# A selective-scan kernel whose per-output adding transfers are issued at other steps and in another order of chunks

## The chip, the cores and the metric

The kernel runs on one core of one Trainium2 chip, as one launch. The metric is the device time of that core in microseconds (us). The kernel before took 9282.05 us, the median of three runs that lay between 9277.97 and 9287.36.

## The reference, cut to what matters

Two layers run one after the other. The first is a linear attention with a layer norm and a residual. The second is a four-direction selective scan with one state per channel, and the change lies in its last part. With 8 images, 256 inner channels (two chunks of 128 partitions) and L = 128 x 128 places, it computes in essence:

```python
xs = jnp.stack([xf, xf[..., ::-1], xt, xt[..., ::-1]], axis=1)       # four directions
dA = jnp.exp(delta * A); xc = dA * xc + delta * u * B; y = xc * C     # scan over L
return y + u * Dv                                                     # the D term
y = y0 + y1 + y2 + y3                    # the directions, turned back to one order
yz = y * silu(z)                         # gate
yn = gamma * (yz - mu) / jnp.sqrt(var + 1e-05) + beta
out = yn @ Wout
```

`u * Dv` is the D term. Because images and directions are mixed by a reshape, the four scans that sum to one output belong to two to four different images, and the D terms of an output depend only on `o // 4`: there are two D sums, each shared by four outputs.

## The kernel before, in words

There are three parts: `layer0`, `layer1_front` and `layer1_scan`. The front computes u, the rows that the scans need, and the two D sums, and leaves them in HBM: u in `ubs`, the rows in `xps`, the gate z in `zs`, the D sums in `gs`. The change touches only `layer1_scan`, which starts at about 4520 us of the profile.

**Units, places and steps.** The scans are cut into 512 units of 1024 positions: for each of 8 outputs o, four scans (four *places*) of 16 units each (`NCH = 16`). A Python function `step(n)` writes out by hand the order in which every engine works, and an order of this kind is kept on every engine (`in_order`). In step n the unit n is weighed and scanned, unit n-1 is multiplied by its C and added to the sum `y`, and the loads of unit n+2 are issued. `y` is a tile of 128 x 2 x 16384 floats that stays in SBUF; the four scans of an output are summed in it. The first place of an output writes `y` (L979), the other three add to it, one half on DVE (L993 or L989, then L1001), the other on GpSimd (L982 on DVE, then L1009).

**Counting steps.** In this text the steps of the last place of an output are numbered 0 to 15, and those of the next output's first place 16 to 31. Step k begins on DVE with the product of the unit before.

**What a step holds.** In the last three places of an output:
- DVE: L993/L989, L1001, L982 and two scans (L959 or L961).
- GpSimd (POOL): two products of u and the softened delta (`weigh`, L951), two additions into `y` (L1009).
- ACT: two softplus (L938) and two exponentials (L942).
- SP issues the loads: rows (L916, L917) and u (`ubt`, L923), both for the unit two steps later.

**Leaving.** While the first place of the next output runs (steps 16 to 31, the `leaving` table), the finished sum leaves in chunks of 1024 positions, one a step: it is multiplied by z (`gate`, L1029, one half on GpSimd in the step before, the other on DVE), squared (L1032), its moments are taken on PE (L1042, L1054), the deviation is made on GpSimd (L1066, L1067), it is projected on PE (L1074), scaled on DVE into a tile `r` (L1080), and stored by SP (`out<-r`, L1084). `r` has two buffers, one for each half of a chunk. So L1080 of one step must wait until the two stores of the step before have landed. SP also issues the loads of z (L1025) in these steps, from step 17 to step 29 for chunks 3 to 15. In the last output there is no next scan, and steps 16 to 32 are a tail with the leaving alone.

**The adding transfers.** The D sum of an output comes from HBM by 16 transfers of 1 MB, each of which adds its data to one chunk of `y`:

```python
def add_d(o, m):
    v = y[:, :, m * CH : m * CH + CH]
    nc.gpsimd.dma_start(v, gs[o // 4].rearrange("c p l -> p c l")[:, :, m * CH : m * CH + CH], accum_op=ALU.add)
```

They are issued by GpSimd (L907) as the last thing of a step, where the table `summed` has an entry. A chunk may be added at any time between the first write of `y` (place 0) and its gate, apart from the units that work on it at that moment; the table decides. Before, the chunk that is the j-th to leave was added in step 3 + (3j + 1) // 2, that is, in steps 3, 5, 6, 8, 9, 11, 12, 14, 15 of the last place and in steps 17, 18, 20, 21, 23, 24, 26 of the next: two in three steps, in the order in which the chunks leave.

Of the kernel before, what the change touches and what calls it, by code (L numbers as in the profile page):

```python
# [32 lines left out]
NCH = L // CH  # L33
# [714 lines left out]
def layer1_scan(ctx: ExitStack, tc, ubs, xps, zs, gs, dtw, dtb, a_log, gamma, beta, w_out, out):  # L748
# [36 lines left out]
    for dst, src, rows in ((wparts, dtw.rearrange("k r d -> r k d"), R), (bparts, dtb.rearrange("o (k d) -> o k d", d=D2), 1)):  # L785
        x = wp.tile([rows, K, D2], F32, name="w32", tag="sp", bufs=2)
        nc.sync.dma_start(x, src)
        q = wp.tile([rows, 3, K, D2], BF16, name="w16", tag="h", bufs=2)
# [298 lines left out]


    leaving, summed, fetched, weighed = {}, {}, {}, {}
    for o in range(B):  # L1090
        n = (o + 1) * K * NCH
        for j in range(NCH):
            e = o, NCH - 1 - j if o % 2 == 1 else j
            leaving[n + j] = e
            fetched[n + j - (2 if j > 2 else NCH + 4)] = e
            summed[n - NCH + 3 + (3 * j + 1) // 2] = e
        n -= K * NCH
        weighed[n + NCH + 1] = n + 2 * NCH
        weighed[n + NCH + 8] = n + 3 * NCH
        if o + 1 < B:  # L1100
            weighed[n + 2 * NCH + 1] = n + 4 * NCH
            weighed[n + 3 * NCH + 1] = n + 5 * NCH
# [104 lines left out]
@with_exitstack  # L1207
def tile_kernel(ctx: ExitStack, tc, a, out):
    dram = ctx.enter_context(tc.tile_pool(name="dram", bufs=1, space=DRAM))
    x1 = dram.tile([B, P, L], F32, name="x1")  # L1210
    ubs = dram.tile([B, 2, NC2, P, L], F32, name="ubs")
    xds = dram.tile([B, R + 2, L], F32, name="xds")
    xps = dram.tile([B, 2, 3, R + 2, L], BF16, name="xps")
    zs = dram.tile([B, NC2, P, L], F32, name="zs")
    gs = dram.tile([2, NC2, P, L], F32, name="gs")
    layer0(
        tc, a["x"], a["L0_conv_w_qkv"], a["L0_conv_w_out"], a["L0_conv_b_out"],
        a["L0_conv_gamma"], a["L0_conv_beta"], a["L1_conv_Win"], x1, zs,
    )
    layer1_front(  # L1220
        tc, x1, a["L1_conv_Win"], a["L1_conv_conv_w"], a["L1_conv_conv_b"], a["L1_conv_Wxproj"],
        a["L1_conv_D_param"], ubs, xds, xps, gs,
    )
    layer1_scan(
        tc, ubs, xps, zs, gs, a["L1_conv_dt_weight"], a["L1_conv_dt_bias"], a["L1_conv_A_log"],
        a["L1_conv_gamma"], a["L1_conv_beta"], a["L1_conv_Wout"], out,
    )
# [40 lines left out]
```

## Time and profile before

| what | value |
|---|---|
| median of three runs | 9282.05 us |
| the profiled execution's own time | 9288.8 us |
| its span, first to last instruction | 9287.0 us |
| DVE busy | 7986.4 us (86%) |
| POOL busy | 7316.7 us (79%) |
| ACT busy | 7097.3 us (76%) |
| adding transfers into `y` (L907) | 128 of 1024 KB, median 10.3 us from issue to landing |
| waits of L1080 for `out<-r` | 80.7 us, 32 times |
| L951 (POOL) | 1024 of 2389 ns |
| L959 and L961 (DVE scans) | 1024 of 2331 and 2330 ns |

The profiled execution took 9288.8 us, of which 1.8 us lie around the span; it is 6.75 us above the median. A line of the profile's list of groups names source line, engine, operation, tiles (written<-read), shapes and count, then busy time and the mean duration, then the idle time before, with what ended it. A line of the timeline gives start and duration in us, engine, line, operation, tiles, count, and in brackets the idle time before it with its releaser. In a table of windows each engine has its busy us and count; the last three columns are the granted TensorE clock, the mean busy share of the 16 DMA engines and GB/s.

### The profile page before, as it was taken

The numbers are of one execution on the slowest core, as the hardware profiler recorded it, in microseconds if no ns is written. First come the engines' busy times: TensorE is split into PE (matmuls) and PEld (weight loads), VectorE is DVE, ScalarE is ACT, GpSimd is POOL, SyncE is SP. The second block draws the span as 40 slices with busy tenths as digits, with TensorE's granted clock in tenths as the row PEclk, the third lists the DMA queues.
The fourth block names the chain that finished last, engine by engine and source line by source line (L and its number), as shares of the span: only waits on it lengthen the run. The fifth ranks groups of instructions, "written<-read, shape, count | busy, mean of one in ns | idle before, by whom it ended". The sixth has DMA issues, their size and how long they took to land.

```text
span 9287.0 us, 91371 instructions
## 1 busy us (share of the span) xinstructions
PE 6364.4 (69%) x24512; PEld 3119.9 (34%) x24512; DVE 7986.4 (86%) x7953; ACT 7097.3 (76%) x8066; POOL 7316.7 (79%) x4684
## 2 busy tenths in 40 slices
PE   8899998988899999999334636346363463643636
PEld 5555555554333333333102304113041140311403
DVE  6667666774799999999799999999999999999996
ACT  5555555658789999999687787888888878888784
POOL 3446444564689988888599899999999989999897
PEclk9999999999999999999555657557575575755757
DMA  1322333223478788888658659577594775957757
GB/s 76 145 84 97 135 120 145 80 100 136 153 247 249 253 244 244 245 245 243 200 156 226 209 180 261 155 222 227 175 269 154 220 221 169 269 161 208 234 167 214
DMA packets 934770, 1750.67 MB, mean 189 GB/s; under 512 B 150228, under 2 KB 376148, under 8 KB 926064
## 3 DMA queue, kind: packets, MB, share of 16 engines
q1 hardware_dynamic: 873328, 1509.92, 48.0%
q0 software_dynamic: 60928, 234.90, 13.6%
q8 instruction: 200, 3.28, 0.1%
q14 instruction: 314, 2.57, 0.1%
HBM read 1052.36 MB, written 692.12 MB: 188 GB/s over the span
## 4 chain that ended last, share of the span: by engine, by line
DVE 36%; PE 5%; DMA 3%; issue 3%; POOL 2%; ACT 1%; DVEq 0%; SPq 0%; POOLq 0%; ACTq 0%
DVE h L961 10%; DVE h L959 10%; DVE y L1001 4%; DVE h L982 4%; DVE px L989 3%; PE px L1074 3%; DMA out<-r 3%; DVE r L1080 2%; DVE px L993 1%; POOL h L951 1%; PE pm L1042 1%; PE pq L1054 0%; PE pc L967 0%; POOL y L1009 0%; POOL z L1029 0%
## 5 line engine op out<-in xcount | busy, mean ns | idle before, releaser
L951 POOL TENSOR_TENSOR h<-ubt,sp 128x1024 f32<-128x1024 f32 x1024 | 2416.6, 2389 | 374.9 <-DMA rows<-xps 92.6
L934 PE MATMUL px<-rows,dtw 128*128 128x512 bf16 x2048 | 956.3, 566 | 2277.8 <-DVE y L1001 1073.2
L534 DVE SCALAR_TENSOR_TENSOR acc<-xb,cw,acc 128x1024 f32<-128x1024 f32 x1024 | 1320.3, 1289 | 133.6 <-ACT xb L502 89.8
L526 POOL TENSOR_TENSOR tap<-tap 128x1024 f32<-128x1024 f32 x512 | 1223.6, 2393 | 243.7 <-ACT tap L524 220.4
L938 ACT ACTIVATE sp<-px 128x1024 f32<-128x1024 f32 x1024 | 1046.7, 1024 | 436.4 <-PE px L934 413.8
L934 PEld LDWEIGHTS <-dtw 128*128 128x128 bf16 x2048 | 168.8, 110 | 3100.8 <-issue 1031.3
L961 DVE TENSOR_TENSOR_SCAN h<-px,h 128x1024 f32<-128x1024 f32 x512 | 1177.4, 2331 | 31.6 <-ACT px L942 15.4
L959 DVE TENSOR_TENSOR_SCAN h<-px,h 128x1024 f32<-128x1024 f32 x512 | 1178.1, 2330 | 22.4 <-POOL h L951 18.5
L1009 POOL TENSOR_TENSOR y<-y,h 128x512 f32<-128x512 f32 x768 | 1159.4, 1553 | 4.3 <-DVE h L982 4.3
L942 ACT ACTIVATE px<-sp,sa 128x1024 f32<-128x1024 f32 x1024 | 1110.4, 1109 | 6.1
L515 PE MATMUL acc<-xi,wt 128*128 128x512 f32 x2048 | 937.6, 600 | 53.6 <-ACT ures L539 53.6
L524 ACT ACTIVATE tap<-xb,cw 128x1024 f32<-128x1024 f32 x768 | 837.3, 1139 | 15.2 <-POOL xb L499 15.1
L282 POOL TENSOR_TENSOR q<-q,qs 128x512 f32<-128x512 f32 x256 | 271.6, 1061 | 697.0 <-DVE qs L281 697.0
L938 ACT ACT_TABLE_LOAD x512 | 656.9, 1283 | 164.6 <-PE px L934 162.7
L942 ACT ACT_TABLE_LOAD x512 | 656.9, 1283 | 9.2
L1074 PEld LDWEIGHTS px<-wg,z 128*128 128x128 f32 x4096 | 588.5, 229 | 113.3 <-issue 107.1
L1074 PE MATMUL px<-wg,z 128*128 128x128 f32 x4096 | 586.9, 312 | 0.0
L967 PE MATMUL pc<-rows,csel 128*128 128x512 bf16 x1024 | 520.0, 588 | 74.8 <-DVE rstd L1062 70.9
L515 PEld LDWEIGHTS acc<-xi,wt 128*128 128x128 f32 x2048 | 374.7, 189 | 573.9 <-issue 411.5
L488 PE MATMUL pxb<-xi,wi 128*128 128x512 f32 x1024 | 495.6, 606 | 2.1 <-ACT xb L497 2.1
L298 ACT ACTIVATE sq<-o 128x512 f32<-128x512 f32 x256 | 161.2, 630 | 420.3 <-DVE o L296 419.1
L1001 DVE TENSOR_TENSOR y<-y,px 128x1024 f32<-128x1024 f32 x384 | 468.5, 1220 | 14.4
(153 smaller groups left out, 15037.9 us busy)
## 6 DMA issues: line engine op xcount, KB each, us to landing
ubt<-ubs SPq DMA_DIRECT2D x1024, 512.0 KB
zs<-z SPq DMA_DIRECT2D x512, 256.0 KB
ubs<-ures SPq DMA_DIRECT2D x256, 512.0 KB
ubs<-turned SPq DMA_DIRECT2D x256, 512.0 KB
z<-zs SPq DMA_DIRECT2D x256, 512.0 KB
y<-gs POOLq DMA_DIRECT2D x128, 1024.0 KB, 10.3
gs<-du POOLq DMA_DIRECT2D x96, 1024.0 KB, 8.6
rows<-xps SPq DMA_DIRECT2D x1536, 60.0 KB
```

The source lines that it names most:

```text
L515: nc.tensor.matmul(acc[:, s, :], wt[:, j, c, :], x, start=(j == 0), stop=(j == len(ON_PE) - 1))
L526: nc.gpsimd.tensor_tensor(sums[n, c], sums[n, c], t, ALU.add)
L534: nc.vector.scalar_tensor_tensor(acc, at(n, c, *d), weight(n, c, *d), acc, ALU.mult, ALU.add)
L934: nc.tensor.matmul(p[:, hf * 512 : hf * 512 + 512], sl.dw[:, c * P : c * P + P], src, start=True, stop=True)
L938: nc.scalar.activation(t, da[n, c], AF.Softplus)
L942: nc.scalar.activation(da[n, c], sp[n, c], AF.Exp, scale=sa[:, sl.s, c : c + 1])
L951: nc.gpsimd.tensor_tensor(h, u, t, ALU.mult)
L959: nc.vector.tensor_tensor_scan(e[:, ::-1], x[:, ::-1], e[:, ::-1], start, ALU.mult, ALU.add)
L961: nc.vector.tensor_tensor_scan(e, x, e, start, ALU.mult, ALU.add)
L1001: nc.vector.tensor_tensor(v, v, ts.pop(n), ALU.add)
L1009: nc.gpsimd.tensor_tensor(v[:, c], v[:, c], h[:, c], ALU.add)
L1074: nc.tensor.matmul(po[:, w, :], z[:, c, w * H : w * H + H], wg[:, c, :], start=(c == 0), stop=(c == NC2 - 1))
```

## The change

Only the table `summed` changes. The chunks that leave 11th to 16th (j = 10 to 15) are added first, then those with j = 0 to 9. With q as the rank in this new order, the step is 1 + 4q // 3. So the adds go out in steps 1, 2, 3, 5, 6, 7 (j = 10 to 15), 9, 10, 11, 13, 14, 15, and 17, 18, 19, 21 (j = 0 to 9): three in four steps. Twelve lie in the last place and four in the next output's first place, where it was nine and seven. The transfers themselves, their number and their size stay, and so does the order on every engine but GpSimd.

```diff
     leaving, summed, fetched, weighed = {}, {}, {}, {}
+    LATE = 10
     for o in range(B):
         n = (o + 1) * K * NCH
         for j in range(NCH):
             e = o, NCH - 1 - j if o % 2 == 1 else j
             leaving[n + j] = e
             fetched[n + j - (2 if j > 2 else NCH + 4)] = e
-            summed[n - NCH + 3 + (3 * j + 1) // 2] = e
+            q = j - LATE if j >= LATE else NCH - LATE + j
+            summed[n - NCH + 1 + 4 * q // 3] = e
```

## The prediction, as it went on record

> **What bounds the kernel now.** I read the page first: busy shares, the chain that ended last, the DMA queues. The change touches only the scan part (from about 4520 us on).
>
> ```profile
> span 9287.0 us, 91371 instructions
> ...
> q1 hardware_dynamic: 873328, 1509.92, 48.0%
> q0 software_dynamic: 60928, 234.90, 13.6%
> ...
> DVE 36%; PE 5%; DMA 3%; issue 3%; POOL 2%; ACT 1%; DVEq 0%; SPq 0%; POOLq 0%; ACTq 0%
> ...
> y<-gs POOLq DMA_DIRECT2D x128, 1024.0 KB, 10.3
> ```
>
> DVE leads the chain, with 3% of DMA behind it. The queue rows give a price. q0 carries 128 + 96 adding transfers of 1 MB: 13.6% of 9287 us is 1263 us of all 16 DMA engines, so one add holds them for 5.64 us. q1 moves 1510 MB in 48.0%, 2.95 us a MB. An added MB costs about twice a plain one.
>
> Next the timeline of POOL and DVE in one last place, to see if an add costs time there.
>
> ```profile
> 4943.66 4.66 POOL L951 TENSOR_TENSOR h<-ubt,sp 128x1024 f32<-128x1024 f32 x2 [1.08 <-DMA rows<-xps]
> 4948.28 2.48 POOL L1009 TENSOR_TENSOR y<-y,h 128x512 f32<-128x512 f32 x2
> 4950.72 1.18 POOL L907 DMA_DIRECT2D y<-gs  x1
> 4951.90 4.69 POOL L951 TENSOR_TENSOR h<-ubt,sp 128x1024 f32<-128x1024 f32 x2
> 4956.53 2.50 POOL L1009 TENSOR_TENSOR y<-y,h 128x512 f32<-128x512 f32 x2
> 4958.96 1.23 POOL L907 DMA_DIRECT2D y<-gs  x1
> 4960.12 4.76 POOL L951 TENSOR_TENSOR h<-ubt,sp 128x1024 f32<-128x1024 f32 x2
> ```
>
> A step there is 8.22 us (start to start), set by DVE: its products follow each other without idle time. POOL needs 4.66 + 2.48 = 7.14 us and idles 1.08. With an add (1.2 us) it fills the step exactly: 8.24 and 8.22 us from L951 to L951. Adds are free for DVE here, but POOL has nothing left.
>
> Then windows: places without adds, a last place with adds, a first place with adds, its end without.
>
> ```profile
> 5245.00:5375.00 130.00, 46.75 (x96) 9.04 (x96) 127.89 (x80) 106.46 (x95) 122.85 (x63) 0.50 0.50 155
> 4935.00:5017.00 82.00, 28.87 (x60) 6.59 (x60) 80.61 (x51) 67.47 (x61) 78.41 (x47) 0.50 0.91 229
> 5046.00:5173.00 127.00, 102.78 (x621) 75.77 (x621) 111.68 (x142) 93.32 (x101) 109.24 (x59) 0.80 0.93 268
> 5200.00:5233.00 33.00, 28.61 (x186) 21.55 (x186) 32.61 (x41) 26.98 (x29) 27.22 (x14) 0.84 0.68 207
> ```
>
> The DMA share is 0.50 without adds, 0.91 and 0.93 with them. In the last place DVE is still 98% busy (80.61 of 82 us), in the first place 88% (111.68 of 127).
>
> What that idle time is, the waits of DVE show (4520 to 9150 us in the first fence, the tail after 9150 in the second) and the timeline shows one of them.
>
> ```profile
> DVE r L1080 <- DMA out<-r: 45.4, 24, 3.6
> DVE h L959 <- POOL h L951: 18.5, 12, 2.2
> DVE h L961 <- POOL h L951: 15.0, 10, 2.2
> ```
>
> ```profile
> DVE r L1080 <- DMA out<-r: 35.3, 8, 6.4
> DVE r L1080 <- PE px L1074: 19.5, 7, 5.0
> ```
>
> ```profile
> 5075.32 2.34 DVE L959 TENSOR_TENSOR_SCAN h<-px,h 128x1024 f32<-128x1024 f32 x1
> 5080.35 2.16 DVE L1080 SCALAR_TENSOR_TENSOR r<-px,rstd,bw 128x128 f32<-128x128 f32 x8 [2.70 <-DMA out<-r]
> 5082.43 2.34 DVE L959 TENSOR_TENSOR_SCAN h<-px,h 128x1024 f32<-128x1024 f32 x1
> ```
>
> L1080 wants its two `r` buffers, whose stores of the step before have not landed. I took each step's length from DVE's timeline in all seven transitions. A step of the first place without such a wait takes 11.28 us; with one it takes 12.4 to 16.0. The waits occur only in the step after an add: in steps 19, 21, 22, 24, 25, 27, never after 19, 22, 25 or from 28 on. Steps 17 to 32 last 197.8, 189.0, 181.1, 184.5, 194.4, 182.4 and 190.5 us; the third has no such wait. Against it the other six lose 16.7 + 8.0 + 3.4 + 13.3 + 1.4 + 9.5 = 52 us (the 45.4 us of waits and what trails them). That is what this change can reach, besides the tail.
>
> **What the Trainium skill says.** DMA: Bandwidth & Descriptors, section "Issuing engines are not separate DMA queues", says that transfers issued by different engines run on the same 16 DMA engines and interleave. The trace agrees: stores issued by SP are late exactly after adds issued by POOL. The same page, "Rules for kernel authors", says that an accumulating transfer reads its destination before it writes; 5.64 us against 2.95 us a MB fits. GPSIMD Engine Reference, section "When to use GPSIMD", gives the descriptors of POOL's transfers to POOL itself; the 1.2 us of L907 on POOL's timeline fit that.
>
> **The change, part by part.** All 128 adds stay; DVE, ACT, PE and SP keep their order.
>
> (1) *Three adds fewer in each first place.* Steps 23, 24 and 26 lose theirs, step 20's goes to step 19. The demand on the DMA engines: steps without z and adds have a share of 0.51 to 0.58 (windows from 5211 to 5233 us; the 0.68 above contains the last z load), some 0.55 x 11.28 = 6.2 us; 1 MB of z adds 2.95, so 9.1 us, and with an add 14.8 us in 11.28. Before, steps 17 to 26 ask 10 x 9.1 + 7 x 5.64 = 130 us in 113: 17.7 us too much, of which 16.7 showed in the first transition and 52 / 7 = 7.5 on average, since landing may lag a little unpunished. After: 91 + 22.6 = 113.6, no excess over the ten steps, but it is bunched, 45.5 + 22.6 = 68 us in the 56.4 us of steps 17 to 21: 11.7 too much.
> By events: waits remain possible in steps 19, 20 and 22. Step 19 waited in two of seven transitions, 2.8 us each: 5.6 us, unchanged. Step 20 now follows a third add in a row, which the trace does not show: between 0 and 7 x 4.4 us (the largest loss in one wait, a step 22 of 15.63 us), I take five of seven at 3.2: 16 us. Step 22 follows an add after a free step, as step 21 did: two at 3.2, about 6 us. Together 28 us stay of 52: 24 us gained, ends 5 and 45. By proportion, 11.7 / 17.7 of 7.5 stay, 35 us of 52: 17 us gained. I take 22.
>
> (2) *The tail.* A free step is 7.35 us (L1062 at 9255.70, 9263.05, 9270.39, 9277.74). Fifteen steps from 9157.00 to 9277.74 take 120.7 us against 110.2; 2.8 us of that lie in the first, before any store. So 7.7 us hang on the seven adds: the 35.3 us of waits mostly replace the waits for PE px. With four of seven adds, 3.3 go. I take 4, ends 0 and 7.7.
>
> (3) *Twelve adds instead of nine in each last place: POOL.* Per add 1.2 us on POOL, covered by its 1.08 idle plus overlap. Queued behind L907 is L951 of the next step, for which DVE's scan waits. The third add in a row leaves POOL up to 3 x 0.04 us late; L951's first half is ready 1.06 us before the scan (done 5011.78, scan 5012.84), so 0. Step 13's add now precedes the two steps with gates on POOL, in which DVE already waits 1.23 and 2.24 us: up to 0.2 us a place, 1 us in all. The cover is POOL's idle time; without it every extra add would cost up to 1.2 us.
>
> (4) *Twelve adds: DMA in the last place.* Without adds 0.50 x 8.22 = 4.1 us a step. Three in four ask 4.1 + 0.75 x 5.64 = 8.3 of 8.22 us. Two in three ask 7.9, a share of 0.96 where 0.91 was measured, so I expect 0.96. Inside three in a row the engines fall 3 x 9.74 - 24.7 = 4.6 us behind, and the free step gives 4.1 back. Late would be `ubt`: issued at 4946.0, its L951 comes two steps later at 4960.1. 14 us hide it, even if two whole adds (11.3 us) ran first. I take 0; not below, because nothing in these steps waits now; the other end is rival D.
>
> (5) *New order.* A chunk added early is used ten steps later by its own unit: 80 us against 10.3 us to land. The chunks j = 0 to 9 are gated three or more steps after their add, 33 us. No cost.
>
> Sum: 22 + 4 - 1 = 25 us, 0.27%. The profiled execution of 9288.8 us would become 9264; the median, 6.75 us below it, 9257. About 0.2% (18.6 us) is what a measurement here can tell from no change.
>
> **The rivals.** *A, forecast:* 9257, 12 to 40 us gained. *B, the waits vanish:* four adds early in the place are absorbed, as the third transition absorbs seven, and 45 to 60 us go: 9230. *C, the waits move:* the three adds in a row make steps 20 and 22 as late as 21 to 27 were; 0 to 12 us: 9276. For it speaks the 11.7 us bunch, against it that five of seven transitions take two adds in a row without a wait in step 19. *D, slower:* the last place, now full, delays `ubt` and rows beyond their 14 us, and L951 and the scan behind it wait. It decides as soon as the 4.6 us of a run of three are not won back by the free step: then each of four runs in eight places costs 1 to 4 us, 32 to 128, less 25: about 9310. Against it: DVE at 98% there now.
>
> **How the numbers follow.** A 0.60, B 0.10, C 0.22, D 0.08. Faster by over 0.2% is most of A and all of B: 0.60; within 0.2%: the rest of A and C: 0.32; slower: 0.08. The range 9230 to 9280 holds B's centre, A and C, and leaves out D and the far side of B.
>
> **What would show it.** Right: steps 23 to 27 at 11.28 us, waits for out<-r in 4520 to 9150 between 15 and 35 us, last-place steps still 8.22 us at a DMA share of 0.96, the tail 3 to 5 us shorter. Wrong: L951 waiting for `ubt` with DVE behind it, last-place steps over 8.3 us, or waits over 45 us, now in steps 20 and 22.

## The result and the profile after

The changed kernel takes 9256.92 us, the median of seven runs (9247.05 to 9265.77), against 9285.92 us before (seven runs, 9277.97 to 9295.03). The ratio is 0.997, with a 95% interval of 0.9959 to 0.9982. The profiled execution took 9261.02 us, its span is 9259.2 us; before it was 9288.8 and 9287.0 us.

The page of the changed kernel, the same lines as before:

```profile
span 9259.2 us, 91316 instructions
...
q1 hardware_dynamic: 873328, 1509.92, 49.4%
q0 software_dynamic: 60928, 234.90, 13.8%
...
y<-gs POOLq DMA_DIRECT2D x128, 1024.0 KB, 10.3
```

The same bytes move, in more packet time (49.4% where it was 48.0%), and an add still takes 10.3 us to land. Now the waits of DVE in the changed kernel: up to 9130 us in the first fence, the tail after 9124 us in the second (us in total, times, longest).

```profile
DVE r L1080 <- DMA out<-r: 23.5, 15, 3.1
DVE h L959 <- POOL h L951: 18.8, 12, 2.2
...
DVE h L961 <- POOL h L951: 14.2, 9, 2.3
```

```profile
DVE r L1080 <- PE px L1074: 27.8, 12, 3.4
DVE rstd L1062 <- ACT mv L1058: 25.4, 14, 6.0
DVE r L1080 <- DMA out<-r: 18.8, 4, 9.7
```

The waits for the stores fell from 45.4 to 23.5 us in the scans and from 35.3 to 18.8 us in the tail. DVE's waits for POOL's product (L951) did not move: 33.5 us before, 33.0 after. Two of the remaining waits, in steps 20 and 22 of the first transition, in DVE's timeline:

```profile
5096.79 2.16 DVE L1080 SCALAR_TENSOR_TENSOR r<-px,rstd,bw 128x128 f32<-128x128 f32 x8 [1.83 <-DMA out<-r]
...
5122.02 2.16 DVE L1080 SCALAR_TENSOR_TENSOR r<-px,rstd,bw 128x128 f32<-128x128 f32 x8 [2.26 <-DMA out<-r]
```

And the windows of a last place and of the first place behind it (busy us and count of PE, PEld, DVE, ACT, POOL, then clock, DMA share, GB/s):

```profile
4940.00:5022.00 82.00, 28.98 (x60) 6.62 (x60) 80.71 (x50) 67.48 (x60) 78.97 (x48) 0.50 0.96 252
5050.00:5177.00 127.00, 98.31 (x657) 72.89 (x660) 118.51 (x146) 99.21 (x108) 111.44 (x60) 0.88 0.91 268
```

DVE is busy for 118.5 of 127 us in the first place where it was 111.7. In the last place the DMA share rose from 0.91 to 0.96 and DVE is as busy as it was.

Read step by step from DVE's timelines, the 27.8 us between the two spans are made up so:

| part | before | after | difference |
|---|---|---|---|
| steps 17 to 32, seven transitions | 1319.7 us | 1292.6 us | -27.1 us |
| tail, first L1062 to last | 120.7 us | 116.5 us | -4.2 us |
| steps 0 to 15, mean of seven outputs | 132.87 us | 132.94 us | +0.5 us in seven |
| start of the step before the first output's step 0 | 4894.3 us | 4899.0 us | +4.7 us |

The last row lies ahead of the first add and its code is unchanged; it varied between 4893.6 and 4899.5 us over the kernels of this study. The remaining 1.7 us lie in step 16 (0.6), in the start of the tail (0.7) and behind DVE's last instruction (0.4).

### The profile page after: what moved, and what is told of

Same layout as the page of the kernel before. It is cut to its first block, busy times and chain, and to the rows that moved or that the text cites. A ratio compares the mean times of both kernels' runs of the same rounds, so it can differ in the third digit from the quotient of the medians.

```text
span 9259.2 us, 91316 instructions
## 1 busy us (share of the span) xinstructions
PE 6337.5 (68%) x24512; PEld 3096.6 (33%) x24512; DVE 7992.0 (86%) x7953; ACT 7099.7 (77%) x8066; POOL 7316.5 (79%) x4684
## 3 DMA queue, kind: packets, MB, share of 16 engines
q1 hardware_dynamic: 873328, 1509.92, 49.4%
## 5 line engine op out<-in xcount | busy, mean ns | idle before, releaser
L951 POOL TENSOR_TENSOR h<-ubt,sp 128x1024 f32<-128x1024 f32 x1024 | 2422.4, 2399 | 348.4 <-ACT mv L1058 124.1
L959 DVE TENSOR_TENSOR_SCAN h<-px,h 128x1024 f32<-128x1024 f32 x512 | 1177.9, 2330 | 21.4 <-POOL h L951 18.8
L1009 POOL TENSOR_TENSOR y<-y,h 128x512 f32<-128x512 f32 x768 | 1159.8, 1559 | 3.8 <-DVE h L982 3.8
L1001 DVE TENSOR_TENSOR y<-y,px 128x1024 f32<-128x1024 f32 x384 | 468.6, 1220 | 14.4
## 6 DMA issues: line engine op xcount, KB each, us to landing
y<-gs POOLq DMA_DIRECT2D x128, 1024.0 KB, 10.3
```

Source lines behind the costliest of these rows:

```text
L951: nc.gpsimd.tensor_tensor(h, u, t, ALU.mult)
L959: nc.vector.tensor_tensor_scan(e[:, ::-1], x[:, ::-1], e[:, ::-1], start, ALU.mult, ALU.add)
L1009: nc.gpsimd.tensor_tensor(v[:, c], v[:, c], h[:, c], ALU.add)
```

## The experiments

The question was whether the 27 us come from the time of the DMA engines beside the stores, from POOL's time for issuing, or from the order of the chunks; and then what limits the number of adds in a last place. Each of the six runs was timed beside the kernel before.

### New times, old order of chunks

```diff
-            summed[n - NCH + 3 + (3 * j + 1) // 2] = e
+            summed[n - NCH + 1 + 4 * j // 3] = e
```

> The new times with the old order of chunks: adds in steps 1, 2, 3, 5, 6, 7, 9, 10, 11, 13, 14, 15, 17, 18, 19, 21, but the j-th to leave is added j-th. Theory (what counts is how many adds lie beside the stores of the leaving, and when): as the changed kernel, some 9257 us, 0.997 of before, waits for out<-r in steps 19, 20 and 22 alone. Rival (the order counts: a chunk added right after its own unit is still in work, or a chunk added late holds its gate): within 5 us of before, 9286, or slower, with waits of L993, L1001 or L1029 for an add.

Measured: 9267.14 us, ratio 0.9974 (0.9963 to 0.9984), which overlaps the interval of the changed kernel. Steps 17 to 32 sum to 1296.7 us (1292.6 in the changed kernel), the tail is 116.5 us in both. So the times make most of the gain, not the order. One small difference stayed: the last places took 133.19 us on average, not 132.94. In this order the adds of steps 1 to 3 go to the chunk that POOL has just written, and L907 stood idle 24 times, 7.8 us in all, where the changed kernel has no such wait. The run with an add in every step shows more of it below.

### Small transfers beside the stores

```diff
-    def add_d(o, m):
-        v = y[:, :, m * CH : m * CH + CH]
+    def add_d(o, m, some=CH):
+        v = y[:, :, m * CH : m * CH + some]
...
-            add_d(*summed[n])
+            o, m = summed[n]
+            add_d(o, m, CH // 8 if n >= (o + 1) * K * NCH else CH)
```

(The source slice shrinks in the same way.)

> The schedule of before, but the adds issued from step 16 on carry the first 128 of the 1024 columns of their chunk only: seven eighths of the D term of the last seven chunks are left out. POOL still issues the same number of transfers with the same number of rows in the same steps. Theory (the DMA engines' time is the cost): the waits for out<-r vanish, 52 us in the seven first places and up to 8 in the tail: about 9226 us. Rival (POOL's 1.2 us of issuing in steps where it is nearly full are the cost): no change from before, 9286 us.

Measured: 9226.85 us, ratio 0.9932 (0.992 to 0.9945), as the theory had it to within 1 us. DVE's waits from 4900 us to the end have no row for `out<-r` any more:

```profile
DVE r L1080 <- PE px L1074: 41.6, 20, 4.9
DVE rstd L1062 <- ACT mv L1058: 36.0, 24, 6.7
DVE h L959 <- POOL h L951: 18.5, 12, 2.2
DVE h L961 <- POOL h L951: 15.1, 10, 2.2
```

The same filter gave 80.7 us for that wait before. POOL still issued every transfer, at a median of 1.25 us each in these steps, so POOL's issuing was not the cost there. The steps 17 to 32 took 179.9 to 181.1 us in all seven transitions. So the data of the late adds cost some 62 us before; the change gained 29.

### The four late adds spread out

```diff
-            summed[n - NCH + 3 + (3 * j + 1) // 2] = e
+            summed[n - NCH + 1 + (4 * j // 3 if j < 12 else 16 + 3 * (j - 12))] = e
```

> Old order of chunks, twelve adds in the last place as in the changed kernel (steps 1, 2, 3, 5, 6, 7, 9, 10, 11, 13, 14, 15), but the other four in steps 17, 20, 23 and 26, every third step. Theory (bunching: two or three adds in a row put the DMA engines behind, one add puts them 3.5 us behind and two free steps of 2.2 us each win it back): hardly any wait for out<-r, below 8 us in all seven transitions, and 9286 - 45 - 6 = about 9235 us. Rival (each add costs the same wherever it stands, 52 us / 49 adds = 1.06 us): 28 adds keep 30 us, as the changed kernel, about 9258 us.

Measured: 9226.24 us, ratio 0.9933 (0.992 to 0.9945): as fast as with the late data nearly gone, though all of it is moved. Steps 17 to 32 take 180.7 to 182.2 us. Against the first run (new times, old order) only the steps of the last four adds differ, and the seven transitions take 1267.8 us instead of 1296.7. So a single add with two free steps behind it costs little: of 28, two made the stores late, 2.4 us of waits in all. The 25 us that the changed kernel still loses in its transitions (1292.6 less seven times 181.1) come from three in a row and the next one after one free step. It is the spacing and not the place of a step: the kernel before also has adds in steps 20, 23 and 26, and there the steps behind them waited in two, two and four of seven transitions, here in none, none and two. The forecast of 9235 us kept 7 us that weren't there.

### An add in every step

```diff
-            summed[n - NCH + 3 + (3 * j + 1) // 2] = e
+            summed[n - NCH + 1 + j] = e
```

> Old order of chunks, one add in every step from 1 to 16: fifteen in the last place, one in step 16, none beside the stores. Theory (DMA engines in the last place are nearly full at three in four): each step asks 4.1 + 5.64 = 9.74 us of the engines in 8.22; the last place stretches by 1.1 to 1.5 us a step, 15 steps, 8 places: 130 to 180 us slower there, less the 60 us of the first places and the tail: 9355 to 9405 us. Rival (only the adds themselves come late, loads keep their place because they have 14 us of time): last-place steps stay 8.22 us, and about 9226 us.

Measured: 9272.07 us, ratio 0.9981 (0.9973 to 0.9989). Neither theory was right. The first places lost all their waits (1265.5 us for the seven) and the tail too (110.2 us), but steps 0 to 15 took 138.76 us, 5.9 us more than before, not the 16 to 22 that the demand on the DMA engines had promised. From step 5 on, steps grew from 8.22 to 8.63 us. POOL's timeline of this run:

```profile
4944.12 1.19 POOL L907 DMA_DIRECT2D y<-gs  x1 [0.30 <-DMA rows<-xps]
4944.90 5.12 POOL L951 TENSOR_TENSOR h<-ubt,sp 128x1024 f32<-128x1024 f32 x2
4949.53 2.92 POOL L1009 TENSOR_TENSOR y<-y,h 128x512 f32<-128x512 f32 x2
4952.74 1.20 POOL L907 DMA_DIRECT2D y<-gs  x1 [0.30 <-DMA rows<-xps]
4953.52 5.13 POOL L951 TENSOR_TENSOR h<-ubt,sp 128x1024 f32<-128x1024 f32 x2
```

POOL hardly rests except for 0.30 us ahead of each L907. The releaser that the trace names was long done; at the first of these, at 4926.85 us, it names POOL's own L1009. In this order every add goes to the chunk that L1009 has just written (DVE's share of it, L1001, had ended 6 us before the L907 at 4944.12), so a new theory was that L907 waits until L1009's data has landed, and that POOL, not the DMA engines, sets the step. The sum fits: 4.66 + 2.48 + 1.2 + 0.30 = 8.64 us.

### An add in every step, in turned order

```diff
-            summed[n - NCH + 3 + (3 * j + 1) // 2] = e
+            summed[n - NCH + 1 + (j + 8) % NCH] = e
```

> As the run with one add in every step from 1 to 16, but in turned order: chunks 8 to 15 of the leaving in steps 1 to 8, chunks 0 to 7 in steps 9 to 16, so that no add follows its own unit's L1009 on POOL. In the run before, L907 stood idle 0.30 us in each step and the step grew to 8.63 us. Theory (POOL, and in it the wait of the add for the addition of its own chunk, set the 8.63 us): steps of 8.22 to 8.35 us, last place 133 to 136 us instead of 138.7, total 9228 to 9250 us. Rival (the DMA engines, asked for 9.74 us a step, set it): last place stays near 138.7, total 9272 us.

Measured: 9223.34 us, ratio 0.9933 (0.992 to 0.9947). Steps 0 to 15 take 133.72 us instead of 138.76. In POOL's timeline the idle time before L907 is gone, in all 128 cases, and the step is 8.22 us from L951 to L951:

```profile
4936.81 4.79 POOL L951 TENSOR_TENSOR h<-ubt,sp 128x1024 f32<-128x1024 f32 x2
4941.43 2.60 POOL L1009 TENSOR_TENSOR y<-y,h 128x512 f32<-128x512 f32 x2
4943.85 1.33 POOL L907 DMA_DIRECT2D y<-gs  x1
4945.03 4.84 POOL L951 TENSOR_TENSOR h<-ubt,sp 128x1024 f32<-128x1024 f32 x2
```

The window of these steps shows POOL at 81 of 81 us and the DMA share at 1.05:

```profile
4936.00:5017.00 81.00, 27.77 (x59) 6.29 (x58) 79.61 (x51) 67.21 (x60) 81.00 (x50) 0.50 1.05 278
```

So the DMA engines carried an add in every step without making DVE wait for a load. The rival is out. A backlog did form: the adds' time to landing rose from 8.9 us in step 1 to 12.6 in step 10 (means of eight outputs), but up to step 13 it rose no further. That L907 waits for the landing of L1009's data is the likely reason of the 0.30 us; what is shown is that it comes with the same chunk and goes with another. What the turned order costs lies where POOL also has the gates: step 15 takes 10.46 us where it took 9.61, and DVE's waits for L951 sum to 41.9 us in this run, 33.5 before.

### No adds near the gates

```diff
-            summed[n - NCH + 3 + (3 * j + 1) // 2] = e
+            summed[n - NCH + (1 + (j + 6) % 12 if j < 12 else 18 + 3 * (j - 12))] = e
```

> Twelve adds in steps 1 to 12 (chunks 6 to 11, then 0 to 5), none in steps 13 to 17, where POOL has gates besides its other work, and the last four in steps 18, 21, 24 and 27. Theory (each 1.2 us add on POOL in steps 14 and 15 is paid by DVE, whose waits for L951 in steps 15 to 17 are 1.3 + 2.2 + 1.1 us): the first two waits fall by 1.2 us each, 2.4 x 8 = 19 us less than the spread run, about 9207 us; the run of twelve adds costs at most 1 us a place. Rival (the gates alone make these waits, or twelve adds in a row overrun the DMA engines): 9226 us or more.

Measured: 9211.84 us, ratio 0.9921 (0.9907 to 0.9934), the lowest median of the study. DVE's waits for POOL's product, from 4900 us on:

```profile
DVE h L959 <- POOL h L951: 8.7, 11, 1.1
DVE h L961 <- POOL h L951: 4.2, 7, 1.1
```

They fell from 33.5 to 12.9 us, 20.6 us, where 19 were expected. Not all of it reached the time. Step 15 takes 8.56 us, 9.69 in the spread run: 9 us in eight outputs. Steps 16 and 17 lost 11 us of these waits, but steps 16 to 32 are only 5.7 us shorter in all. The median is 14.4 us below that of the spread run; but the two were timed apart, and against the kernel before, timed beside each, they gain 72.6 and 62.8 us, 9.8 us apart. The edit does more than keep clear of the gates: the turned order alone was worth 2 us above (133.19 to 132.94 us, eight times), and the four lone adds come one step later. The transition after the first output, with 184.4 us for its steps 17 to 32, again lost time to stores: the lone adds of steps 18 and 24 made them 1.95 and 1.39 us late. So an add that stands alone costs little, not always nothing.

## Why the prediction was right, point by point

The forecast was 9257 us and 25 us gained; the medians give 9256.92 us and 29.0 us. That the time agrees to 0.1 us is luck: the gain was 4 us larger, and the kernel before, with 9285.92 us over seven runs, 3.9 us slower than the 9282.05 from which the forecast started.

- **Step (1), first places.** 22 us were taken, 24 by counting events; 27.1 us came. The events fell where the prediction had put them: step 19 waited in two of seven transitions, step 20 in seven (one of them for only 0.43 us), step 22 in three. Steps 23 to 27 are at 11.14 to 11.60 us. By excess over 181.07 us, 25 us stay of 52 where the count of events had said 28. The run with small transfers shows that the DMA engines' time was the cause, the spread run that the bunch was.
- **Step (2), the tail.** 4 us taken, 4.2 measured (120.7 to 116.5 us), but the agreement is luck. 2.8 of the 4.2 us lie in the tail's first step, which the prediction had set apart because no store lies before it: it took 10.14 us and takes 7.35. PE's projection makes the difference, the first line before, the second after:

```profile
9156.61 6.61 PE L1074 MATMUL px<-wg,z 128*128 128x128 f32 x32
...
9133.52 3.82 PE L1074 MATMUL px<-wg,z 128*128 128x128 f32 x32
```

The granted TensorE clock was 0.54 from 9157 to 9163 us before and 1.00 from 9134 to 9137.5 us after. The run with small transfers, whose tail has hardly any added data, keeps the long first step (10.01 us); all runs with other times have the short one. Why the clock rises earlier there stays open. What hangs on the stores fell only from 7.7 to 6.3 us, 1.4 instead of 4: one step takes 13.5 us, the next 8.5, one 6.4 and the others 7.35.

- **Step (3), POOL.** Nothing was expected but up to 1 us in all at steps 14 and 15; steps 0 to 15 grew by 0.07 us an output. The reason was right for this change: at most three adds in a row, and none to the chunk that L1009 has just written. The runs with an add in every step show what is behind it: 1.2 us of L907 fits by a hair, and with another 0.30 us it doesn't. One thing the step took as given: "Adds are free for DVE here" does not hold where POOL has gates. Both kernels have adds in steps 14 and 15; without adds in steps 13 to 17 the last place takes 131.83 us, 1.1 less than in the changed kernel, and DVE's waits for L951 fall by 20 us.
- **Step (4), DMA in the last place.** A share of 0.96 was expected and 0.96 measured. But the price was too high, and only the scaling by the measured 0.91 made up for it. Per added transfer 5.64 us of all engines were taken; an add in every step raised the share from 0.50 to 1.05, which is 0.55 x 8.22 = 4.5 us. Rival D was further off than its working had it: even an add in every step was carried. That the packets' time, from which 5.64 us comes, contains waiting is likely but not shown; for it speaks that the same bytes of q1 took 48.0% of 9287 us before and 49.4% of 9259 us after, 116 us more.
- **Step (5), order.** No cost for the new order, and it is slightly better than the old: 132.94 against 133.19 us for the same times. The step named only the chunk's next use; that the add itself might have to wait for what comes ahead of it was not considered.
- **Rivals.** C (the waits move) happened in part: all seven transitions now have a late store in step 20, where none had one before; but step 22 waited in three of seven only. B (the waits vanish) is what the spread run did, with four adds that stand apart.

## What to carry to other kernels

In this kernel the data of a background transfer cost time only where something with little slack shared the DMA engines, here the stores behind two buffers. Before counting how many such transfers lie there, look at how they stand: four adds three steps apart cost next to nothing, and four almost in a row cost 3.6 us a transition. And when a transfer is moved into a stage that looks free, look at the engine that issues it: in the last places GpSimd set the limit, not the DMA engines, and keeping adds away from its gates was worth some 10 us more.

## What was not expected of the hardware

- An adding transfer issued by GpSimd right behind GpSimd's own write of the same chunk stood 0.30 us; for another chunk it did not stand (128 of 128 adds against none). In a step that is full to within 0.1 us this is 5 us in each last place (138.76 against 133.72 us).
- The DMA engines reached a share of 1.05 at 278 GB/s with an add in every step, and DVE waited for no load. In the first places the stores were late at 0.93. So the share alone did not tell whether something waits.
